# Attention in a convolution network: values for four key tiles at a time, and filler ahead of the logits in the steps between

## The chip, the core and the metric

The kernel runs on one core of a Trainium2 chip. The metric is the time of one execution on the device in microseconds (us), given as the median of several runs. The core has five engines, each with its own instruction queue: TensorE (PE; its weight loads are listed apart as PEld), VectorE (DVE), ScalarE (ACT), GpSimd (POOL) and SyncE (SP), which here issues nearly all transfers. Matmul results go to PSUM, everything else on the core is held in SBUF.

## What is computed

Eight images of 512 channels and 32 x 32 pixels pass through two layers, in fp32. The first holds nearly all the work: a 1x1 convolution, two blocks of 3x3 convolution and attention, and a closing 1x1 convolution over all intermediate results. The second is a 1x1 convolution whose weights are masked and permuted. Cut to what matters:

```python
def bot_attention(x, qkv_w, rw, rh):          # 4 heads of 64 channels, hw = 1024 pixels
    qkv = conv2d(x, qkv_w, 0).reshape(b, 3, HEADS, HD, hw)
    q, k, v = (qkv[:, 0], qkv[:, 1], qkv[:, 2])
    r = (rw + rh).reshape(1, HEADS, HD, hw)
    logits = jnp.einsum('bhdi,bhdj->bhij', q, k + r) * HD ** (-0.5)
    a = jax.nn.softmax(logits, axis=-1)
    out = jnp.einsum('bhij,bhdj->bhdi', a, v)
    return out.reshape(b, c, h, w)

t = cbs(x, cv1_w, cv1_bn, 0)                  # cbs: convolution, batch norm, silu
ys = [t[:, :C], t[:, C:]]                     # C = 256
for i in range(N):                            # N = 2 blocks
    yi = ys[-1]
    z = cbs(yi, m_cv1_w[i], m_cv1_bn[i], 1)   # 3x3
    z = bot_attention(z, m_qkv_w[i], m_rw[i], m_rh[i])
    z = jax.nn.silu(bn_eval(conv2d(z, m_cv2_w[i], 0), m_cv2_bn[i]))
    ys.append(yi + z)
return cbs(jnp.concatenate(ys, axis=1), cv2_w, cv2_bn, 0)

x = x + _L0_conv_ref(_gn(x), ...)             # _gn: group norm
x = x + _L1_conv_ref(_gn(x), ...)
```

## The kernel before

**Units.** Attention is cut into 64 units: 16 slots (an image and a block each, two images in turn) of four units, one for each pair of heads and half of the queries (512). A unit has `KT` = 8 key tiles of 128 keys. For each tile and head:

- `logits` (L487): a matmul with 64 rows for each of the two heads into a PSUM bank `lg`, a ScalarE copy of it to the SBUF tile `st` (L500), and on VectorE the running maximum `mx` (L505), read from the same bank.
- `top` (L507) transposes the maxima on TensorE (`mt`) and reduces them on VectorE; `spread` (L516) spreads them over a PSUM tile `mb` by eight more transposes.
- `soften` (L523): VectorE adds `mb` to `st`, ScalarE takes the exponential in place, and POOL sums it into `acc`, in two instructions.
- `values` (L533): a matmul for each head, with 64 output columns, added up over the eight tiles in the one bank `po`.
- `finish` (L545): the denominators `den` by a matmul with ones from `acc`, copied to `rb` by ScalarE; `divide` (L554) takes reciprocals and multiplies `po` into `q`, in two parts.

A group of `logits` uses 64 rows of TensorE's array for each head, and a group of `values` or `den` 64 columns; all other matmuls use it as 128 by 128.

**The loop** (L981 to L1036). A unit `u` goes through its eight tiles in four steps of two (`t` = 0, 2, 4, 6). Each step softens two tiles of `u`, takes the values of the two tiles softened a step before, and computes two tiles of the logits of the next unit, `nxt`. The last two tiles' values come after the loop. The reciprocals of the unit before lie in step 0.

**Filler.** The convolutions of other images and blocks fill TensorE between these pieces. `slot_filler` lists a slot's share of them as generators with estimated costs; `advance` takes pieces until the share `(base + ...) / steps` of the slot's total is reached, where `steps` is 40, ten for each unit. A piece is 1.33 or 1.72 us of the planner's time, or a little less. `clock.tick` moves the planner's clock, which decides when timed VectorE work (the transforms of the 3x3 convolution, L244, the group norms) is written into the program. The additions of `soften`, the maxima and the transforms keep their written order on VectorE (`in_turn`, L182); otherwise the framework orders each engine's instructions by its own plan of when they are ready.

**Buffers.** PSUM has eight banks here: two for `mb`, one for `po`, and five in the pool `ps_f` for logits, transposes, denominators and filler. `st` has ten buffers: eight for the unit under way and two for the next one's first logits; later logits use those that `values` and POOL's sums have released. The pool `wp` has four buffers for convolution weights (`weights`, L80), `wt` three for temporaries of the transforms. `kvp` has three for `k` and three for `v`. Batch norm parameters, the positions `rw` and `rh`, and the inputs of the second layer's mask have tiles of their own (L86 to L89), `tri` too (L658).

Of the kernel before, what the change touches and what calls it, by code (L numbers as in the profile page):

```python
# [15 lines left out]
F32 = mybir.dt.float32  # L16
# [6 lines left out]
P = 128  # L23
NB = 8
CT = 4
IT = 2
F = 32
HW = F * F
HALF = 512
NBLK = 2  # L30
HD = 64
NG = 16
KT = 8
NGR = 17

BN_CV1, BN_CV2, BN_M1, BN_M2, BN_ALL = 0, 4, 8, 12, 16
# [3 lines left out]
def conv_preact_kernel(ctx: ExitStack, tc: tile.TileContext, x, cv1, cv2, mcv1, qkv, mcv2, bn, rw, rh, conv, s_in, t_in, out):  # L40
# [3 lines left out]
    def pool(name, bufs, **kw):  # L44
        return ctx.enter_context(tc.tile_pool(name=name, bufs=bufs, **kw))

    const = pool("const", 1)
    dram = pool("dram", 1, space=bass.MemoryType.DRAM)
    small = pool("small", 2)
    qp = pool("qp", 2)  # L50
    kp_ = pool("kvp", 3)
    stp = pool("stp", 10)
    one = pool("one", 1)
    wp = pool("wp", 4)
    gx = pool("gx", 4)
    wm = pool("wm", 1)
    gy = pool("gy", 4)
    gr = pool("gr", 2)
    tp = pool("tp", 3)
    wt = pool("wt", 3)  # L60
    ps_m = pool("ps_m", 1, space=PSUM)
    ps_o = pool("ps_o", 1, space=PSUM)
    ps_f = pool("ps_f", 5, space=PSUM)
# [7 lines left out]
    def half_tile(name):  # L71
        return tp.tile([P, HALF], F32, tag="t", name=name)
# [10 lines left out]
        return t  # L83


    bn_sb = const.tile([P, 4, BN_ALL], F32, name="bn_sb")  # L86
    s_sb = const.tile([P, 2, CT, NG], F32, name="s_sb")
    rw_sb = const.tile([P, NBLK, IT, F], F32, name="rw_sb")
    rh_sb = const.tile([P, NBLK, IT, F], F32, name="rh_sb")  # L89


    w_m1 = [[dram.tile([P, IT, IT, 3, P], F32, name=f"w_m1_{i}_{r}") for r in range(6)] for i in range(NBLK)]
# [515 lines left out]
    def last_weights():  # L608
# [46 lines left out]

        yield

        tri = small.tile([P, P], F32, tag="tri", bufs=1, name="tri")  # L658
        nc.gpsimd.affine_select(
            out=tri, in_=ones, pattern=[[1, P]], compare_op=ALU.is_gt, fill=0.0, base=0, channel_multiplier=-1  # L660
        )
# [28 lines left out]
        for i in range(CT):  # L690
# [5 lines left out]
            t = half_tile(f"wl_{i}")  # L696
# [35 lines left out]
    clock = Clock()  # L732
# [210 lines left out]
    first, second = images[:2]  # L943
# [16 lines left out]
    bg.prepare()  # L960
    first.transform(0, 0.0, 0.0)
    side = last_weights()
    for n, us in enumerate(first.conv3(0)):
        clock.tick(us)
# [16 lines left out]
    for s in range(len(slots)):  # L981
        needed, total, todo = slot_filler(s)
        state = {"done": 0.0}

        def filler():
            for us, g in todo:
                start = state["done"]
                for cost in g:
                    clock.tick(cost)
                    state["done"] += cost  # L990
                    yield

                state["done"] = max(state["done"], start + us)

        fill = filler()

        def advance(share):
            goal = max(share * total, min(1.0, share / 0.74) * needed + 0.1)
            while state["done"] < goal:
                if next(fill, "end") == "end":  # L1000
                    break

        steps = 4 * (KT + 2)
        for j in range(4):
            u = units[4 * s + j]
            nxt = units[4 * s + j + 1] if 4 * s + j + 1 < len(units) else None
            base = j * (KT + 2)
            u.top()
            clock.tick(0.9)
            advance((base + 1) / steps)  # L1010
            u.spread()
            clock.tick(0.9)
            advance((base + 2) / steps)
            if before:
                before.finish()
                clock.tick(0.9)
            for t in range(0, KT, 2):
                u.soften(t)
                if before and t == 0:
                    before.divide(1)  # L1020
                u.soften(t + 1)
                if t:
                    u.values(t - 2)
                    u.values(t - 1)
                    clock.tick(2.0)
                if nxt:
                    nxt.logits(t)
                    nxt.logits(t + 1)
                    clock.tick(2.0)
                advance((base + 4 + t) / steps)  # L1030
            u.values(KT - 2)
            u.values(KT - 1)
            clock.tick(2.0)
            before = u
        for _ in fill:
            pass  # L1036
# [59 lines left out]
```

## Time and profile before

| what | value |
|---|---|
| median of 3 runs | 3273.07 us |
| lowest and highest of them | 3271.97, 3283.51 us |
| profiled execution, own time | 3278.47 us |
| its span, first to last instruction | 3276.7 us |
| granted TensorE clock | 0.99 |
| HBM read, written | 317.42 MB, 79.69 MB |

The profile is of one execution. Its times are in us, unless in ns. A row of a group of instructions shows the line, the engine and operation, output and inputs, the shape and number; then the busy time of the engine and the mean ns of one instruction; then the engine's idle time just before such instructions, and what ended it. A row of the timeline shows a start, a duration, and the instructions merged in it. TensorE's ends are modelled and overlap the next start a little, so starts are what is compared. By fortieths of the span the clock is at nine tenths or more throughout. The units run from about 184 us, when the first logits start, to 3145 us; before lies the preparation of weights and the first two images, after it the last image's convolutions.

### The profile page before, as it was taken

What the parts mean: (1) busy time and instruction counts of PE and PEld (TensorE: products, weight loads), DVE (VectorE), ACT (ScalarE), POOL (GpSimd) and SP (SyncE); (2) the same over time, 40 slices, a digit from 0 to 9 for tenths busy, and PEclk for the clock granted to TensorE, in tenths of its full rate; (3) what the DMA queues carried; (4) which work ended last, traced back from release to release, by engine and by line L of the source; (5) the groups of instructions that cost most, each with busy time, mean ns of one, the idle gap of its engine ahead of it and who ended that gap; (6) DMA issues with size and microseconds to landing.
All of it is one profiled execution on the core that took longest, in us unless ns stands there. A gap on an engine that the chain in (4) does not pass through costs nothing.

```text
span 3276.7 us, 33257 instructions
## 1 busy us (share of the span) xinstructions
PE 3159.1 (96%) x11716; PEld 1538.0 (47%) x11716; DVE 2045.9 (62%) x2717; ACT 1756.6 (54%) x2369; POOL 1219.1 (37%) x971
## 2 busy tenths in 40 slices
PE   7999999998999999999999999999999999999998
PEld 3645345353545445354545445354445444453343
DVE  5436566666666575767666675767656676666642
ACT  3245765854545655644545555644655554646631
POOL 2104433335334343344334343444334433444420
PEclk9999999999999999999999999999999999999999
DMA  8752352330323241423323341423333341423366
GB/s 292 275 171 71 119 170 94 116 106 20 121 98 106 75 148 55 161 84 106 122 98 105 104 144 54 161 84 108 124 105 108 101 141 49 160 71 116 111 217 205
DMA packets 142007, 399.30 MB, mean 122 GB/s; under 512 B 13072, under 2 KB 14352, under 8 KB 141840
## 3 DMA queue, kind: packets, MB, share of 16 engines
q1 hardware_dynamic: 141120, 396.94, 36.1%
q8 instruction: 93, 1.52, 0.2%
q14 instruction: 74, 0.61, 0.1%
q10 hardware_dynamic: 720, 0.23, 0.0%
HBM read 317.42 MB, written 79.69 MB: 121 GB/s over the span
## 4 chain that ended last, share of the span: by engine, by line
PE 69%; DVE 11%; issue 5%; ACT 4%; DMA 4%; POOL 1%; POOLq 0%; SPq 0%; ACTq 0%; DVEq 0%
PE cv L175 14%; PE m L297 12%; PE po L537 11%; PE lg L494 10%; PE qk L175 6%; PE l L175 5%; PE v L389 3%; DVE st L525 3%; PE mt L513 2%; PE m L175 2%; DVE rb L556 2%; DVE mx L505 2%; PE den L549 2%; PE mb L521 2%; DMA x<-in_x 1%
## 5 line engine op out<-in xcount | busy, mean ns | idle before, releaser
L531 POOL TENSOR_TENSOR sum<-sum,st 128x512 f32<-128x512 f32 x768 | 973.9, 1299 | 771.5 <-ACT st L526 771.5
L526 ACT ACTIVATE st<-st 128x1024 f32<-128x1024 f32 x512 | 534.3, 1056 | 471.4 <-DVE st L525 464.8
L505 DVE TENSOR_TENSOR mx<-mx,lg 128x512 f32<-128x512 f32 x768 | 479.3, 681 | 434.1 <-ACT st L500 433.6
L500 ACT COPY st<-lg 128x512 f32<-128x512 f32 x1024 | 528.1, 594 | 246.1 <-PE lg L494 189.9
L525 DVE TENSOR_TENSOR st<-st,mb 128x1024 f32<-128x1024 f32 x512 | 604.2, 1213 | 79.8 <-PE mb L521 79.8
L297 PE MATMUL m<-plane,w_m 128*128 128x256 f32 x2304 | 534.0, 386 | 18.0 <-DVE z L351 8.3
L494 PE MATMUL lg<-q,k 64*128 64x512 f32 x2048 | 534.6, 618 | 10.4 <-ACT rb L551 3.3
L537 PE MATMUL po<-st,v 128*64 128x512 f32 x2048 | 509.5, 609 | 17.2 <-ACT st L526 11.4
L297 PEld LDWEIGHTS m<-plane,w_m 128*128 128x128 f32 x2304 | 431.4, 191 | 142.7 <-issue 40.8
L531 POOL TENSOR_TENSOR sum<-st,st 128x512 f32<-128x512 f32 x128 | 162.2, 1288 | 834.1 <-ACT st L526 712.0
L175 PE MATMUL cv<-y,w_cv 128*128 128x512 f32 x1024 | 466.5, 600 | 4.9 <-DVE mx L505 2.1
L494 PEld LDWEIGHTS lg<-q,k 64*128 64x128 f32 x2048 | 188.9, 186 | 346.2 <-issue 236.5
L175 PEld LDWEIGHTS cv<-y,w_cv 128*128 128x128 f32 x1024 | 185.5, 190 | 252.0 <-issue 231.6
L537 PEld LDWEIGHTS po<-st,v 128*64 128x64 f32 x2048 | 125.2, 136 | 327.6 <-issue 231.6
L556 DVE RECIPROCAL rb<-rb 128x256 f32<-128x256 f32 x128 | 216.1, 1725 | 66.0 <-ACT rb L551 66.0
L175 PE MATMUL cv<-x,w_cv 128*128 128x512 f32 x512 | 242.2, 622 | 12.3 <-DVE mx L505 4.1
L175 PE MATMUL l<-x,w_l 128*128 128x512 f32 x512 | 235.2, 604 | 9.6 <-DVE mx L505 6.2
L175 PE MATMUL qk<-z,w_qkv 128*128 128x512 f32 x512 | 234.2, 600 | 1.6 <-DVE mx L505 1.6
L514 DVE TENSOR_REDUCE nm<-mt 128x4 f32<-128x512 f32 x128 | 83.0, 685 | 221.5 <-PE mt L513 221.2
L130 ACT ACT_TABLE_LOAD x122 | 156.5, 1283 | 14.7 <-PE m L175 6.4
L175 PEld LDWEIGHTS cv<-x,w_cv 128*128 128x128 f32 x512 | 97.0, 197 | 138.7 <-issue 112.1
L175 PEld LDWEIGHTS l<-x,w_l 128*128 128x128 f32 x512 | 93.3, 191 | 133.6 <-issue 106.5
(144 smaller groups left out, 2342.1 us busy)
## 6 DMA issues: line engine op xcount, KB each, us to landing
w_m<-w_m SPq DMA_DIRECT2D x96, 768.0 KB, 4.4
w_cv<-in_cv SPq DMA_DIRECT2D x90, 512.0 KB, 3.5
y<-y SPq DMA_DIRECT2D x64, 512.0 KB, 4.7
x<-in_x SPq DMA_DIRECT2D x56, 512.0 KB, 5.2
y<-y SPq DMA_DIRECT2D x64, 256.0 KB, 3.6
k<-r SPq DMA_DIRECT2D x32, 512.0 KB, 3.8
res<-y SPq DMA_DIRECT2D x32, 512.0 KB, 4.2
xr<-in_x SPq DMA_DIRECT2D x32, 512.0 KB, 4.3
```

What stands on the lines that cost most here:

```text
L130: nc.scalar.activation(dst, src, AF.Silu, bias=bn_b[:, col : col + 1], scale=bn_s[:, col : col + 1])
L175: nc.tensor.matmul(ps, w, moving, start=(n == 0), stop=(n == len(terms) - 1))
L297: nc.tensor.matmul(ps[:, ts(co, 256)].rearrange("p (t x) -> p t x", x=F), w[:, co, c, dx], u[:, 9 * c : 9 * c + 8, dx : dx + F], start=(j ...
L389: nc.tensor.matmul(ps[:, ts(j, P)], z[:, c, ts(4 * j4 + j, P)], w[:, c, 512 + P * hp : 512 + P * hp + P], start=(c == 0), stop=(c == IT - 1),)
L494: nc.tensor.matmul(lg[h], self.k[r, ts(t, P)], self.q[r, self.hp, ts(self.half, HALF)], start=True, stop=True)
L500: nc.scalar.copy(st[:, h], lg[h])
L505: in_turn(nc.vector.tensor_tensor(self.mx[:, h], so_far[:, h], lg[h], ALU.max))
L525: in_turn(nc.vector.tensor_tensor(st, st, flat(self.mb), ALU.add))
L526: nc.scalar.activation(st, st, AF.Exp)
L531: nc.gpsimd.tensor_tensor(self.acc[:, h], so_far[:, h], self.st[t][:, h], ALU.add)
L537: nc.tensor.matmul(self.po[HD * h : HD * h + HD], self.v[:, t, ts(h, HD)], self.st[t][:, h], start=(t == 0), stop=(t == KT - 1),)
L556: nc.vector.reciprocal(self.rb[:, r], self.rb[:, r])
```

## The change

Values are taken in two groups of four tiles: tiles 0 to 3 in step `t` = 4, tiles 4 to 7 after the last step. In the other steps an additional `advance` stands between `soften` and `logits`, to the share `base + 2.8 + t`; the `advance` after the logits keeps its goal. `st` gets twelve buffers, `wp` three instead of four, `wt` two instead of three. The small parameters move into one tile `par`, which takes one of the three `k` buffers.

```diff
-    stp = pool("stp", 10)
+    stp = pool("stp", 12)
-    wp = pool("wp", 4)
+    wp = pool("wp", 3)
-    wt = pool("wt", 3)
+    wt = pool("wt", 2)
...
-    bn_sb = const.tile([P, 4, BN_ALL], F32, name="bn_sb")
-    s_sb = const.tile([P, 2, CT, NG], F32, name="s_sb")
-    rw_sb = const.tile([P, NBLK, IT, F], F32, name="rw_sb")
-    rh_sb = const.tile([P, NBLK, IT, F], F32, name="rh_sb")
+    par = kp_.tile([P, HW], F32, tag="k", name="par")
+
+    def param(first, shape):
+
+        return par[:, first : first + P].rearrange("p (a b c) -> p a b c", b=shape[0], c=shape[1])
+
+    s_sb = param(0, (CT, NG))
+    rw_sb = param(128, (IT, F))
+    rh_sb = param(256, (IT, F))
+    bn_sb = par[:, 512 : 512 + 4 * BN_ALL].rearrange("p (a b) -> p a b", b=BN_ALL)
...
-        tri = small.tile([P, P], F32, tag="tri", bufs=1, name="tri")
+        tri = par[:, 384:512]
...
                 u.soften(t + 1)
-                if t:
-                    u.values(t - 2)
-                    u.values(t - 1)
-                    clock.tick(2.0)
+                if t == KT // 2:
+                    for key in range(KT // 2):
+                        u.values(key)
+                    clock.tick(4.0)
+                else:
+
+                    advance((base + 2.8 + t) / steps)
                 if nxt:
                     nxt.logits(t)
                     nxt.logits(t + 1)
                     clock.tick(2.0)
                 advance((base + 4 + t) / steps)
-            u.values(KT - 2)
-            u.values(KT - 1)
-            clock.tick(2.0)
+            for key in range(KT // 2, KT):
+                u.values(key)
+            clock.tick(4.0)
```

## The prediction

> **What bounds the kernel now.** I read the page's busy totals first, then its chain, then the groups of TensorE by line and form, then TensorE's timeline.
>
> ```profile
> PE 3159.1 (96%) x11716; PEld 1538.0 (47%) x11716; DVE 2045.9 (62%) x2717; ACT 1756.6 (54%) x2369; POOL 1219.1 (37%) x971
> ...
> PE 69%; DVE 11%; issue 5%; ACT 4%; DMA 4%; POOL 1%; POOLq 0%; SPq 0%; ACTq 0%; DVEq 0%
> ```
>
> TensorE is busy 96% of the span, and no other engine passes 62%. The chain runs through TensorE for 69%. So a microsecond counts here if TensorE loses it: as idle time, or inside its busy time.
>
> ```profile
> L494 PE MATMUL lg<-q,k 64*128 64x512 f32 x2048 | 534.6, 618 | 10.4 <-ACT rb L551 3.3 <-ACT y L130 3.1 <-ACT st L500 3.0
> L297 PE MATMUL m<-plane,w_m 128*128 128x256 f32 x2304 | 534.0, 386 | 18.0 <-DVE z L351 8.3 <-DVE mx L505 6.2 <-DMA w_m<-w_m 2.8
> L537 PE MATMUL po<-st,v 128*64 128x512 f32 x2048 | 509.5, 609 | 17.2 <-ACT st L526 11.4 <-DVE q L558 5.8
> ...
> L513 PE MATMUL mt<-ident,mx 128*128 128x128 f32 x512 | 73.3, 288 | 10.7 <-DVE mx L505 10.7
> ```
>
> The last column is TensorE's idle time before a group, by who ended it. Values (po) waited 17.2 us, logits (lg) 10.4, the transposes of the maxima (mt) 10.7. Adding all such idle times of the timeline between 250 us, where the units run, and the end gives 85 us.
>
> ```profile
> 1596.36 1.94 PE L537 MATMUL po<-st,v 128*64 128x512 f32 x8
> 1598.23 1.99 PE L494 MATMUL lg<-q,k 64*128 64x512 f32 x8
> 1600.15 5.45 PE L297 MATMUL m<-plane,w_m 128*128 128x256 f32 x24
> 1605.53 1.94 PE L537 MATMUL po<-st,v 128*64 128x512 f32 x8
> ```
>
> Each matmul is two records. A filler group of twelve 128x512 records takes 5.35 us from its start to the next group's (1609.31 to 1614.66), one of eight 3.63 (1528.12 to 1531.75), so a record is 0.43 us of work (I use 0.427), and one of 256 columns half of it, 0.213; the two heads of values or logits share the array, so eight records are 4 x 0.427 = 1.71 us of work. Starts are 1.87 us apart from values to logits (0.16 over), 1.92 from logits to filler (0.21 over), 5.38 from filler to values against 24 x 0.213 = 5.12 (0.26 over). So every change of tile shape costs 0.16 to 0.26 us, unseen as idle time. Beyond that, groups get broken up:
>
> ```profile
> 1500.81 1.12 PE L494 MATMUL lg<-q,k 64*128 64x512 f32 x2
> 1501.86 1.08 PE L537 MATMUL po<-st,v 128*64 128x512 f32 x4
> 1502.87 1.12 PE L494 MATMUL lg<-q,k 64*128 64x512 f32 x2
> 1503.94 1.08 PE L537 MATMUL po<-st,v 128*64 128x512 f32 x4
> 1504.95 1.13 PE L494 MATMUL lg<-q,k 64*128 64x512 f32 x4
> ```
>
> One step's values and logits take from 1500.81 to 1506.01, 5.20 us where 3.79 is usual: lone heads no longer share the array.
>
> **What the Trainium skill says.** "TensorEngine Tiling (Array Packing)", Key Properties: changing the tiling mode drains TensorE, changing only the tile doesn't. The trace agrees: 0.16 to 0.26 us per change, as above. "PSUM — Partial Sum Buffer", Specifications, gives 8 banks per partition; the kernel's pools take all eight (mb two, po one, five shared), and logits of two tiles need four of the five. "TensorE: Matmul & The Clock Gate", the specification table, has VectorE and ScalarE work as strict queues. The trace agrees: at 1543.28 values start late (0.69 us) behind VectorE's reciprocals and `q`, and logits' maxima come after those.
>
> **The change part by part.** There are 64 units (16 slots of four); I cost 63, since the last has no logits beside it.
>
> *Fewer, longer values groups.* Work is the same. Per unit two filler→values changes (0.25 each) and two values→logits changes (0.16) go: -0.82. Step 0 loses denominator→logits (0.15, from 1.01 between starts against 0.85) and gains denominator→filler (taken as 0.16, the price of leaving the same tile shape). Steps 0, 2 and 6 gain filler→logits: 0.21 (filler of six 128x256 records at 1539.74, logits at 1541.23: 1.49 against 1.28). Added 0.79, removed 0.97: -0.18 a unit. With 0.23 for filler→values it is -0.14; I take -0.16 x 63 = **-10 us**. The bounds are -0.4 (the filler ahead of logits in step 0 comes out empty) and 0: -25 to 0 us. I expect it not empty: 0.8 of 40 steps of some 103 us is 2.06 us, above the largest single piece of 1.72.
>
> *Waits of values.* Values of tiles 0 to 3 now stand in step 4, one step (about 9 us by the timeline) or two behind their exponentials, and po is written a step later than `divide`, which frees it. All 17.2 us of waits before po go. Of logits' waits, those on `rb` (filler now lies after the denominators) and on `st` (its buffer is freed two steps ahead instead of just before, also by POOL's sums, for which ScalarE waited 41.3 us) are 6.3 us. Filler's waits on the maxima are 20.9 us over its groups, on `st` 4.0: a filler that follows logits finds all banks held. The filler there shrinks from 2 shares to 1.2 in three of four steps, so half goes: 12.5. Sum 36; TensorE reaches VectorE's next backlog sooner, so I take five sixths: **-30 us**, bounds -36 and -12 (every wait on VectorE comes back later).
>
> *Broken groups.* In the timeline logits run straight into values 24 times (0.5 over), into logits after a hold 11 times (0.7), values into filler 18 times (0.38): 12 + 8 + 7 = 27 us over the sum of their work, of which ordinary changes would keep a little. They come from values or a bank not being ready in the planned order. Values no longer are late; logits' banks may be. **-15 us**, bounds -25 and +10.
>
> *Logits straight after filler.* This is new: until now 1.87 us of values lay between filler and logits in 191 cases, in which ScalarE or VectorE could empty filler's last bank. Logits need four of five banks; where filler stops in mid-sum it holds one, and the bank that it finished 1.3 to 1.7 us before must be empty when the fourth logits matmul starts, 0.85 us later. ScalarE has the step's exponentials (1.06 us each) and perhaps a 1.28 us table load ahead of that. Filler stops so at perhaps a quarter of the 3 x 63 = 189 places (sums of two quanta half the time, of four a quarter, none where a bank is one quantum). 45 places by about 0.3 us: **+15 us**, bounds 0 and +95 (0.5 us at all 189). What stands behind a waiting logits matmul on TensorE is everything.
>
> *Maxima to transposes.* Filler between logits(6,7) and the next `top` shrinks from 2 shares (5.15 us) to 1.2 (3.1), values grow by 1.7: some 0.35 us less for ScalarE's four copies (0.59) and VectorE's four maxima (0.68). mt waited three times by 3.6 us. **+4 us**, bounds -5 and +15. Timed VectorE work (the transforms) falls due around other instructions, since the planner's clock moves by 4.0 twice instead of by 2.0 four times; it is within these bounds.
>
> *Buffers and queues.* No DMA is added; filler's loads and stores move with its pieces on SP by at most one step's share, and POOL's sums keep their place in POOL's queue. Three weight buffers instead of four let a load start one weight later. From SP's issue times of the 250 weight loads, what remains is two weights of use: about 9 us at least while units run, against 4.4 us median to landing, so it stays covered; after 3145 us, without units, 6 us at two places: **+1 us**, up to +8. Two `wt` tiles instead of three are written and read by VectorE in its own order: nothing. The parameters' tile holds one of three `k` buffers until the positions and ranks are made, before the loop takes the third: nothing. Twelve `st` tiles may let the weights' preparation run ahead (TensorE waited 2.8 us for them at 78 and 85 us): **-1 us**.
>
> Sum: -10 - 30 - 15 + 15 + 4 + 1 - 1 = **-36 us**. The profiled execution took 3278.47 us (span 3276.7, 1.8 around it); it becomes 3242.5. The median of the runs is 5.4 below the profiled one: 3273.07 - 36 = **3237 us**.
>
> **Rivals.** *Nearly all of it comes through:* waits -36, broken groups -25, changes -10, logits after filler +5: -66, **3207 us**. For it speaks that few waits need more than a microsecond of slack; against, that VectorE at 62% carries the same work. *The gain is given back:* a third of the waits, and the new bank waits at +20, broken groups unchanged: -10 - 12 + 20 + 4 = +2, **3275 us**. For it: most of the 85 us is filler waiting on itself (z, y, m2s) and on maxima. *Slower:* one mechanism, filler's last bank at the head of logits. Its place is the 189 filler→logits passages; against the other terms' -51 us it decides from a mean of 0.27 us on. At 0.45 us it costs 85: +34, **3307 us**. For it: logits waited 3.1 us once for `y`, and filler→logits occurs only 11 times before, so its price is hardly seen; against: those 11 show no idle time. *The change doesn't do what it says*, the pieces ahead of logits being empty: changes -25, but logits of tiles 0 and 2 come within 5.2 us with no values between, bank waits +30, so -25 - 25 - 10 + 30 = -30, **3243 us**, not to be told from the forecast by time.
>
> **How the numbers follow.** A measurement here can tell 0.5%, 16 us, from no change. Forecast 0.46 (its own range 3215 to 3257); nearly all 0.16; empty pieces 0.06; given back 0.14; slower 0.18. Faster by over 16 us: 0.46 + 0.16 + 0.06 = 0.68, within 0.14, slower 0.18. Leaving a tenth at each end: 3198 to 3295.
>
> **What would show it.** After: values in about 128 groups instead of 269, mostly of 16 records; po's idle near nothing; filler's idle on mx about 10 us; TensorE's busy total down by some 20 us or more at unchanged instruction counts. Wrong, if logits' idle grows beyond 20 us, with `y`, `cv2s`, `x2r` or `m2s` named, if lone heads of logits are more frequent, or if mt's idle goes beyond 25 us.

## The result, and the profile after

| what | before | after |
|---|---|---|
| median, same comparison, 7 runs each | 3276.68 us | 3290.81 us |
| ratio, 95% interval | | 1.0042 (1.0027 to 1.0056) |
| span of the profiled execution | 3276.7 us | 3288.6 us |
| first transposes of maxima (first unit ready) | 218.2 us | 231.7 us |
| from there to the last unit's transposes | 2894 us | 2892 us |
| from those to the end | 164.4 us | 164.6 us |

The change costs 14 us, 0.42%, where 36 us less was forecast. The three stretches of the last rows are read from TensorE's timeline. The whole difference of the spans, 11.9 us, lies ahead of the first transposes (+13.5). The loop, which was to become about 36 us shorter, took the same time.

The busy totals and the chain of the page after:

```profile
PE 3173.9 (97%) x11716; PEld 1547.1 (47%) x11716; DVE 2059.5 (63%) x2717; ACT 1749.0 (53%) x2361; POOL 1231.0 (37%) x971
...
PE 70%; DVE 10%; issue 6%; ACT 5%; DMA 2%; POOL 1%; SPq 0%; POOLq 0%; DVEq 0%; ACTq 0%
```

TensorE has the same 11,716 instructions and is busy 14.8 us longer, 7.5 of it ahead of the first transposes (196.1 us before, 203.7 after). Its groups by line and form, after (line numbers are six higher than before in this part of the file):

```profile
L500 PE MATMUL lg<-q,k 64*128 64x512 f32 x2048 | 546.8, 619 | 12.1 <-DVE mx L511 3.9 <-ACT cv2s L136 3.9 <-DVE x2r L477 1.5
L303 PE MATMUL m<-plane,w_m 128*128 128x256 f32 x2304 | 535.9, 385 | 6.9 <-DVE x2r L477 2.4 <-DMA w_m<-w_m 2.0 <-DVE z L357 1.2
L543 PE MATMUL po<-st,v 128*64 128x512 f32 x2048 | 500.3, 603 | 15.8 <-DVE q L564 11.4 <-ACT st L532 4.4
...
L181 PE MATMUL cv<-x,w_cv 128*128 128x512 f32 x512 | 242.3, 620 | 19.7 <-ACT y L136 6.8 <-DVE mx L511 5.3 <-DMA w_cv<-in_cv 5.3
...
L181 PE MATMUL m<-q,w_m 128*128 128x512 f32 x256 | 125.1, 626 | 10.8 <-ACT m2s L136 10.8
...
L519 PE MATMUL mt<-ident,mx 128*128 128x128 f32 x512 | 70.1, 280 | 0.0
```

Idle time went where it was looked for and came in elsewhere. The transposes (`mt`) wait no more (10.7 before), and the values' wait on `st` fell from 11.4 to 4.4 us. But the values' wait on `q`, the division that frees `po`, rose from 5.8 to 11.4, and the matmuls `m<-q`, which waited 4.0 us before and only for `st`, now wait 10.8 us, all for `m2s`: ScalarE's copy of filler's finished bank. `cv<-x` shows a wait for a weight load (5.3 us) that it did not have. The rows of these two before:

```profile
L175 PE MATMUL cv<-x,w_cv 128*128 128x512 f32 x512 | 242.2, 622 | 12.3 <-DVE mx L505 4.1 <-ACT y L130 4.0 <-ACT x L165 2.4
L175 PE MATMUL m<-q,w_m 128*128 128x512 f32 x256 | 121.4, 614 | 4.0 <-ACT st L500 4.0
```

For the loop, from the first to the last unit's transposes, I split what TensorE's records show beyond their own work into three. A record's work is 0.427 us for 512 columns, and half of that for logits, values and denominators, of which two share the array.

- *Idle* is the sum of its waits in the timeline.
- *Half clock* is time lost because the granted clock fell to 0.5. The traces show such stretches, 3.41 us long or a multiple of that; in the trace after, a 128x512 record takes 0.853 us in them (median) and 0.429 elsewhere. I count half of TensorE's busy time in these stretches, which is an estimate. The profile counts it as busy, and a fortieth of the span averages it away. In this stretch after, ahead of the loop, the mean granted clock is 0.70 (the columns are length, busy time and number of instructions for PE, PEld, DVE, ACT and POOL, the clock, and DMA):

```profile
208.40:214.00 5.60, 5.51 (x10) 2.21 (x12) 3.85 (x6) 2.70 (x7) 0.00 (x0) 0.70 0.14 51
```

- *Changes and breaks* is all the rest: shape changes and broken groups.

| in the loop | idle | half clock | changes and breaks | sum |
|---|---|---|---|---|
| before | 83.9 us | 25.0 us | 236.7 us | 345.6 us |
| after | 75.6 us | 16.7 us | 253.3 us | 345.6 us |

Changes and breaks grew by 17 us, and that repeats: a second execution of the kernel before has 81.8, 23.0 and 237.8 us, and one with the same loop as the changed kernel ("weights later" below) 72.8, 13.6 and 254.7. What grew are groups of logits or values with an odd number of matmuls, so that one head goes without its partner: 30 before, 80 after. After, a group of 6 records takes 1.93 us, as long as one of 8 (1.92), and one of 2 takes 1.05, as long as one of 4 (1.07). So 50 more of them cost some 21 us (50 x 0.427), while 60 fewer changes of shape at 0.2 us give back 12. Both are estimates from these figures; 8 of the 17 us stay unexplained.

By cause, the idle time on `mx` fell from 32.7 to 15.5, and on the exponentials from 11.4 to 4.4. On ScalarE's three copies of filler (`m2s`, `y`, `cv2s`) it rose from 8.3 to 25.6, and on `q` from 5.8 to 11.4. So 24 us of such waits went, and 23 us of others came.

Where in a unit the sum stands (the first stretch starts with the transposes of the maxima; each ends with the named logits, and the last with the start of the next transposes):

| stretch of a unit, all units | before | after |
|---|---|---|
| transposes to the first step's logits | 81.5 us | 103.2 us |
| to the second step's | 74.5 us | 61.9 us |
| to the third's | 65.2 us | 71.5 us |
| to the fourth's | 71.4 us | 69.8 us |
| to the next transposes | 53.1 us | 39.1 us |

The last stretch, in which four tiles' values stand instead of two, gains 14 us, and the second 13. The first, where filler now comes ahead of the logits, loses 22, and the third, with four tiles' values, 6.

TensorE's timeline in the middle of the loop, after, shows what became of the groups:

```profile
1036.19 3.70 PE L181 MATMUL m<-q,w_m 128*128 128x512 f32 x8
1039.83 1.98 PE L500 MATMUL lg<-q,k 64*128 64x512 f32 x6
1042.81 1.04 PE L543 MATMUL po<-st,v 128*64 128x512 f32 x2 [1.00 <-DVE q L564]
1043.78 1.12 PE L500 MATMUL lg<-q,k 64*128 64x512 f32 x2
1044.84 1.98 PE L181 MATMUL m<-q,w_m 128*128 128x512 f32 x4
...
1054.05 3.65 PE L543 MATMUL po<-st,v 128*64 128x512 f32 x14
```

This is step 0 of a unit: filler, then logits. Only three of the four logits matmuls run (x6, two records each), and they take as long as four. Then comes one matmul of the values that belong to step 4, drawn forward by two steps. It waits 1.00 us for the division of the unit before, and so does everything behind it. The fourth logits matmul follows alone, and the values at 1054.05 have 14 records left instead of 16. In the program's order on TensorE, whole groups of four tiles' values are 99 of 128, and values come in 163 groups (271 before); changes of shape fell only from 936 to 876.

### The profile page after: what moved, and what is told of

Its sections match the earlier page's. It is cut to its first block, busy times and chain, and to the rows that moved or that the text cites. A ratio compares the mean times of both kernels' runs of the same rounds, so it can differ in the third digit from the quotient of the medians.

```text
span 3288.6 us, 33211 instructions
## 1 busy us (share of the span) xinstructions
PE 3173.9 (97%) x11716; PEld 1547.1 (47%) x11716; DVE 2059.5 (63%) x2717; ACT 1749.0 (53%) x2361; POOL 1231.0 (37%) x971
## 4 chain that ended last, share of the span: by engine, by line
PE 70%; DVE 10%; issue 6%; ACT 5%; DMA 2%; POOL 1%; SPq 0%; POOLq 0%; DVEq 0%; ACTq 0%
PE m L303 13%; PE cv L181 12%; PE po L543 12%; PE lg L500 11%; PE qk L181 6%; PE l L181 5%; PE v L395 3%; DVE st L531 3%; DVE rb L562 2%; PE m L181 2%; PE mt L519 2%; PE den L555 2%; PE mb L527 2%; ACT st L532 1%; DVE mx L511 1%
## 5 line engine op out<-in xcount | busy, mean ns | idle before, releaser
L531 DVE TENSOR_TENSOR st<-st,mb 128x1024 f32<-128x1024 f32 x512 | 604.7, 1214 | 76.8 <-PE mb L527 76.8
L500 PE MATMUL lg<-q,k 64*128 64x512 f32 x2048 | 546.8, 619 | 12.1 <-DVE mx L511 3.9
L543 PE MATMUL po<-st,v 128*64 128x512 f32 x2048 | 500.3, 603 | 15.8 <-DVE q L564 11.4
L543 PEld LDWEIGHTS po<-st,v 128*64 128x64 f32 x2048 | 139.6, 137 | 332.1 <-issue 279.5
L562 DVE RECIPROCAL rb<-rb 128x256 f32<-128x256 f32 x128 | 216.3, 1726 | 53.2 <-ACT rb L557 53.1
```

The source lines that it names most:

```text
L500: nc.tensor.matmul(lg[h], self.k[r, ts(t, P)], self.q[r, self.hp, ts(self.half, HALF)], start=True, stop=True)
L531: in_turn(nc.vector.tensor_tensor(st, st, flat(self.mb), ALU.add))
L543: nc.tensor.matmul(self.po[HD * h : HD * h + HD], self.v[:, t, ts(h, HD)], self.st[t][:, h], start=(t == 0), stop=(t == KT - 1),)
L562: nc.vector.reciprocal(self.rb[:, r], self.rb[:, r])
```

## The experiments

Each was compared with runs of the kernel before on the same chip; a ratio below 1 is faster than before. The profiled execution of a kernel can lie some us from its median, and loop times are of that one execution. "Changes" are changes of tile shape in the program's order on TensorE, from the first values on. The time lost in the loop is given as idle + half clock + changes and breaks. Two executions of the kernel before differ by 3 us in the loop.

### Which part costs the time

Four kernels: the kernel before with all the buffer changes and the single parameters' tile; with the third weight buffer alone; the changed kernel without the additional filler; and the changed kernel with values in twos as before, but with the additional filler.

```diff
 e1  # the buffers and `par` as changed; values and filler as before
 e2  # before, and only
-    wp = pool("wp", 4)
+    wp = pool("wp", 3)
 e3  # changed, without
-                else:
-                    advance((base + 2.8 + t) / steps)
 e4  # changed, with
+                if t != KT // 2:
+                    advance((base + 2.8 + t) / steps)
+                if t:
+                    u.values(t - 2)
+                    u.values(t - 1)
```

> Kernel before with all buffer changes (twelve st, three weight buffers, two wt, the parameters in one tile), but its own order of values and filler. In the changed kernel the first maxima's transposes start at 231.7 us instead of 218.2, and from there to the end the two kernels differ by under 2 us. Theory A: the loss is the start, and the buffers cause it: first transposes at 228 to 232 us, time 10 to 14 us over before (3286 to 3291). Rival R: the start's lateness is chance (TensorE's clock warming up at other moments), and the loop's new order costs the time: first transposes at 218 to 222 us, time within 4 us of before.

> Kernel before with three weight buffers instead of four, nothing else. Theory A, with the third buffer as the cause: the second w_cv load of the stage before the loop is issued after 155 us instead of at 121, TensorE waits some 5 us for it, first transposes at 225 to 232 us, time 7 to 14 us over before. Theory B (the shared tile of parameters, or twelve st, shift the start): first transposes within 3 us of 218, time within 3 us of before.

> Changed kernel without the additional filler ahead of the logits: values in fours, all filler after the logits. Its program has 822 changes of tile shape on TensorE from the first values on, against 876 in the changed kernel and 936 before. If changes of shape at 0.2 us set the loop's time: 54 x 0.2 = 11 us below the changed kernel, about 3280, that is 23 us below before once the start's 13 us are taken off. If logits that follow each other within 5 us wait for banks (what the filler was put in to avoid): logits' and filler's idle on maxima up by 20 to 60 us and time 3295 to 3340.

> Changed buffers, values in twos as before, but the filler split, with a piece ahead of values and logits in three of four steps. 983 changes of shape against 936 before: 47 x 0.2 = 9 us over the kernel that has the new buffers alone. If filler ahead of the logits removes waits on maxima and on rb, as forecast (12 to 19 us), it comes out 3 to 10 us below that kernel; if it only cuts groups up, 9 to 15 us above.

| kernel | median us | ratio (95%) | first transposes | loop | lost in the loop | changes |
|---|---|---|---|---|---|---|
| before | 3278.25 | 1 | 218.2 | 2894 | 83.9 + 25.0 + 236.7 | 936 |
| buffers | 3278.03 | 1.0002 (0.9992 to 1.0011) | 230.3 | 2885 | 77.7 + 19.2 + 239.8 | 936 |
| `wp` alone | 3280.09 | 1.0005 (0.9996 to 1.0014) | 231.5 | 2885 | 75.0 + 24.9 + 236.7 | 936 |
| values grouped | 3289.68 | 1.0041 (1.0025 to 1.0057) | 230.5 | 2893 | 83.2 + 15.7 + 246.9 | 822 |
| filler split | 3303.14 | 1.0076 (1.0054 to 1.0097) | 231.4 | 2907 | 83.2 + 23.7 + 253.2 | 983 |

The late start is the third weight buffer's: it alone moves the first transposes by 13 us. Where it comes from stands in the profile after. SyncE's queue, after:

```profile
160.96 0.32 SPq L78 DMA_DIRECT2D w_m<-gf  x1
161.37 0.94 SPq L78 DMA_DIRECT2D r<-r  x2
162.41 1.14 SPq L78 DMA_DIRECT2D w_cv<-in_cv  x1
```

and TensorE's timeline, after:

```profile
156.85 7.03 PE L181 MATMUL cv<-x,w_cv 128*128 128x512 f32 x16
169.14 5.06 PE L181 MATMUL cv<-x,w_cv 128*128 128x512 f32 x8 [5.25 <-DMA w_cv<-in_cv]
174.03 0.28 PE L152 MATMUL gm_a<-mv_a,gmat 128*128 128x4 f32 x2
```

The second `w_cv` of this stage is issued at 162.41 us, behind the stores of the second block's weights (`w_m<-...`). The kernel before issues that load at 121.44:

```profile
121.44 0.33 SPq L78 DMA_DIRECT2D w_cv<-in_cv  x1
```

TensorE then stands for 5.25 us, and its next eight records take 4.89 us, from 169.14 to 174.03, where eight take 3.63 otherwise. TensorE was behind by 4.6 us at 156.85 already; the kernel before started this group at 152.21:

```profile
152.21 10.46 PE L175 MATMUL cv<-x,w_cv 128*128 128x512 f32 x24
```

Up to there the changed kernel had 13.65 us at half clock and the kernel before 6.83, which by itself costs some 3.4 of the 4.6 us. A later wait of 2.07 us, 0.28 longer than the same one before, is followed by eight slow records (1.7 us more). Together 13.1 of the 13.5 us.

But the late start doesn't decide the time by itself, as I had expected it to (3286 to 3291 us with all the buffer changes): the kernels with the old order of the loop win 6 to 9 us back in it (2885 against 2894 and 2891) and end where they were. In both, idle time is lower. With `wp` alone neither half clock nor changes and breaks differ from before. With all the buffer changes less time passes at half clock, and values wait 5.8 us on `st` instead of 11.4:

```profile
L543 PE MATMUL po<-st,v 128*64 128x512 f32 x2048 | 510.7, 610 | 11.7 <-ACT st L532 5.8 <-DVE q L564 5.8
```

(The line numbers are those of the changed kernel here, too.) The grouping alone has 114 changes of shape fewer than before and still loses 10 us more to changes and breaks (246.9 us), so it pays elsewhere what it saves in regular changes. The additional filler alone is the worst of the four, 25 us above the kernel with the buffers, where I had expected at most 15: it was the part of the change that I had counted as a gain for the waits.

### Does the order cause it, or the start

Four kernels: before once more, for the spread; the changed kernel and the kernel before with the logits' and values' matmuls kept in their written order by scheduling edges, which add no instruction; and the changed kernel with the preparation of the second block's weights, whose stores stood ahead of the load, moved behind the filler that uses it.

```diff
 e5, e7
+        def pe_in_turn(instruction):  # each logits and values matmul after the one written before it
+            if pe_turn:
+                tc.add_manual_dep(instruction.ins, pe_turn.pop().ins.name, IN_ORDER, reason="order of TensorE")
+            pe_turn.append(instruction)
 e6
-    transform_weights(1)
     positions(1)
     clock.run(bg.take(7.0, force=True))
+    transform_weights(1)
```

> The kernel before once more, for a second profile. The kernels with three weight buffers had their first transposes at 230 to 232 us, the one profile of before at 218.2, but their medians equal that of before. If the 12 us at the start are a property of the buffers: 217 to 220 us again, and the loop (first to last transposes) 3058 less 159, that is 2894 us as before. If the one profile was an early chance: 225 to 232 us, and a loop near 2885 us.

> Changed kernel, with the matmuls of logits and values kept among themselves in the order in which they are written (a scheduling edge from each to the next, no wait on the chip, since all are on TensorE). In the changed kernel the plan draws values forward into logits that have no bank yet: 14 logits groups of one matmul, values before `divide` has freed po. Theory: these broken groups ate the gain. Shape changes go from 876 to 843, po's idle on q from 11.4 to under 3 us, time 15 to 30 us below the changed kernel (3261 to 3276). Rival: the places are short of a bank either way, and TensorE waits there instead: logits' idle up by 10 to 20 us, time within 8 us of the changed kernel.

> The kernel before with the same edges. Shape changes 936 to 911. If broken groups cost as the working had it (0.4 to 0.7 us each, 43 of them): 8 to 15 us below before, 3263 to 3270. If TensorE waits there instead: within 5 us of before.

> Changed kernel with the second block's weights prepared after the convolution that stands before the loop, so that the load of its second w_cv is queued ahead of the weights' stores on SP. The program of the loop on TensorE is the same. If the start counts: TensorE's wait of 5.3 us on w_cv goes, first transposes 6 to 10 us earlier (222 to 226), time 6 to 10 us below the changed kernel (3281 to 3285). If a late start is made up for later in the loop, as it looked in the kernels with buffers alone: time within 4 us of the changed kernel.

| kernel | median us | ratio (95%) | loop | lost in the loop | changes |
|---|---|---|---|---|---|
| before again | 3277.43 | one run | 2891 | 81.8 + 23.0 + 237.8 | 936 |
| changed, in order | 3293.41 | 1.0051 (1.0036 to 1.0066) | 2893 | 83.6 + 21.1 + 241.6 | 843 |
| before, in order | 3266.83 | 0.9968 (0.9955 to 0.9981) | 2880 | 87.0 + 22.2 + 222.2 | 911 |
| changed, weights later | 3281.14 | 1.0013 (1.0006 to 1.0021) | 2888 | 72.8 + 13.6 + 254.7 | 876 |

The groups of the changed kernel in order:

```profile
L508 PE MATMUL lg<-q,k 64*128 64x512 f32 x2048 | 544.4, 619 | 22.8 <-DVE mx L519 11.6 <-ACT m2s L136 3.5 <-ACT cv2s L136 3.0
...
L551 PE MATMUL po<-st,v 128*64 128x512 f32 x2048 | 490.9, 603 | 0.0
...
L181 PE MATMUL cv<-x,w_cv 128*128 128x512 f32 x512 | 245.0, 626 | 25.1 <-ACT y L136 9.8 <-DVE mx L519 6.6 <-DMA w_cv<-in_cv 5.5
...
L181 PE MATMUL m<-q,w_m 128*128 128x512 f32 x256 | 125.0, 626 | 14.1 <-ACT m2s L136 14.1
```

No values are drawn forward, and they don't wait at all (0.0). Changes and breaks fall by 12 us, but in their place logits wait 22.8 us, and filler longer on `y` and `m2s`. The time is no better than the changed kernel's own (the intervals overlap). So keeping the order is not enough to have the gain: what was lost in broken groups is lost in waiting instead.

In the kernel before the same edges gain 10 us: there its values still wait (27.6 us in the row), but fewer groups are broken (10 with a lone head instead of 30), and changes and breaks fall by 14.5 us.

```profile
L502 PE MATMUL lg<-q,k 64*128 64x512 f32 x2048 | 521.4, 618 | 6.5 <-ACT rb L559 3.3 <-ACT y L130 3.1
L545 PE MATMUL po<-st,v 128*64 128x512 f32 x2048 | 508.2, 611 | 27.6 <-DVE q L566 13.9 <-ACT st L534 13.4
```

With the weights later that load is issued at 149.12 us, TensorE doesn't wait for it, the first transposes come at 221.7 us, and the changed kernel is 9.5 us faster than it was against the kernel before (14.1 to 4.4 us over it in median, each in its own comparison). About two thirds of the measured loss is the start; the loop still gains little or nothing by the change (2888 us in this execution, against 2894 and 2891 before).

### Can another order have the gain

Four kernels, all with the weights later: the second step's additional filler with a later goal, so that logits are spaced evenly; the additional filler taken to the end of a sum, so that it holds no half-done bank when logits start; the order of before with the changed buffers, in order; and values grouped without the additional filler, in order.

```diff
 e13
-                    advance((base + 2.8 + t) / steps)
+                    advance((base + (3.5 if t == 2 else 2.8) + t) / steps)
 e10
-                    advance((base + 2.8 + t) / steps)
+                    advance((base + 2.8 + t) / steps, whole=True)  # on to the last matmul of a bank; marks in the filler are left out here
 e11  # e1 with pe_in_turn and the weights later
 e12  # e3 with pe_in_turn and the weights later
```

> The changed kernel with the early w_cv load (late weights), and the filler ahead of step 2's logits taken to share base + 5.5 instead of base + 4.8; the filler after them still goes to base + 6. So the logits of tiles 0 and 2 are on average 1.8 us further apart and those of 2 and 4 nearer by as much. In the changed kernel the mean distance fell from 8.9 to 7.7 us, and TensorE's idle time between logits 0 and 4 rose from 23 to 38 us over the loop. Theory: logits that follow within some 8 us find ScalarE and VectorE still at work on the step before, and filler's banks wait behind that. Then the idle between logits 0 and 4 falls by 5 to 15 us, and the time is 5 to 15 us below the kernel with the late weights alone (3266 to 3276). Rival: the wait moves to logits 4; time within 4 us of it.

> The changed kernel with late weights, with filler ahead of logits taken on to the end of a sum, so that it holds no bank over the logits (and often uses up the filler meant for after them). Theory of the forecast: a bank held by a half-finished sum is what logits lack; then logits' idle and the groups cut up fall and the time is 5 to 15 us below the kernel with late weights alone. Rival: the plan itself still has 17 lone logits matmuls (14 before), so it isn't the held bank; with no filler after logits, maxima and exponentials are waited for: 5 to 40 us above.

> Order of the kernel before (values in twos, no filler ahead of logits) with the new buffers, the late weights, and the edges that keep logits and values in written order. If the gains add up: first transposes at 220 to 223 us, loop 2876 to 2880 us, time 3255 to 3263. If the buffers' shorter loop was only the making up for the late start: loop as with the edges alone, 3264 to 3268.

> Values in fours without filler ahead of logits, late weights, and the edges: 800 changes of shape, the fewest of all (911 in the order before with edges). If changes of shape set the time: 111 x 0.2 = 22 us below the order before with edges, about 3240. If banks do, as the experiment with values in fours has it: 3270 to 3285.

| kernel | median us | ratio (95%) | lost in the loop | changes |
|---|---|---|---|---|
| spaced evenly | 3296.36 | 1.0045 (1.0030 to 1.0060) | 82.9 + 21.5 + 244.0 | 850 |
| whole sums | 3290.23 | 1.0031 (1.0018 to 1.0043) | 76.0 + 23.0 + 256.3 | 821 |
| old order, new buffers, in order | 3271.13 | 0.9970 (0.9960 to 0.9979) | 86.9 + 22.8 + 225.0 | 911 |
| grouped, in order | 3288.30 | 1.0027 (1.0015 to 1.0038) | 85.4 + 24.8 + 240.6 | 800 |

The forecast had named half-done banks at the head of logits as the danger. Removing them (whole sums) doesn't help, so they aren't the cause alone; but this kernel also has less filler left after the logits. Spacing moves the wait: between the third and the fourth step's logits idle time grows from 18 to 42 us while others fall. The old order, kept, is as good with the changed buffers as without them, 9 us under the kernel before. The orders with values grouped, with 800 to 876 changes, lose 341 to 355 us in the loop, the old order kept loses 331 and 335 with more changes (911). So the number of changes doesn't set the time. All of these kernels have a pool of five banks, of which two tiles' logits take four; whether that is what the grouped orders lack is tested next.

### Is it the banks

First by leaving work out. In these four kernels the maxima are not spread and not subtracted (`st` is added to itself, so that VectorE keeps its instruction), and `mb` has no banks. The two banks stay unused (n5) or go to the shared pool (n7); each as the kernel before and as the changed kernel with the weights later, so that in these pairs the buffers differ too.

```diff
-            in_turn(nc.vector.tensor_tensor(st, st, flat(self.mb), ALU.add))
+            in_turn(nc.vector.tensor_tensor(st, st, st, ALU.add))
-            u.spread()
-    ps_m = pool("ps_m", 1, space=PSUM)
-    ps_f = pool("ps_f", 5, space=PSUM)
+    ps_f = pool("ps_f", 7, space=PSUM)   # 5 in n5
```

> Leaves out that the maxima are spread and subtracted (the eight transposes into mb, and mb as the addend: `soften` adds st to itself, so VectorE's instruction stays), which frees mb's two banks; they stay unused here, five banks in the shared pool. Order of the kernel before. It is the measure for the other three. 64 x 0.97 us of transposes go: 3190 to 3230.

> The same cut in the changed kernel with late weights, five shared banks. Both theories: within 10 us of the order before with five banks, as with the whole kernels (4 us apart).

> The same cut, order of the kernel before, with the two freed banks in the shared pool: seven. The plan has 899 changes of shape against 906. Theory that banks hold the loop up: idle of TensorE on maxima falls, 5 to 20 us below five banks. Theory that VectorE's and ScalarE's work between softmax and logits does it: within 5 us.

> The same cut in the changed kernel with late weights, seven shared banks. The plan has 798 changes of shape against 825, and 126 whole groups of four tiles' values against 105. Theory that the shortage of banks took the forecast gain: 20 to 40 us below the order before with seven banks (fewer changes and waits come through), idle on m2s, y, cv2s, q and maxima under half. Rival, that the gain is gone for another reason (VectorE and ScalarE are behind whatever the banks): within 8 us of the order before with seven banks.

Then with nothing left out. The maxima are spread through two banks of a shared pool of seven, ScalarE copies them to SBUF as bf16, and VectorE adds them from there; once with the changed order, once with that of before (both with the changed buffers and the weights later).

```diff
-            self.mb = pair(ps_m, "mb", f"mb_{self.name}")
+            self.mb = mbp.tile([P, 2, HALF], mybir.dt.bfloat16, tag="mb", name=f"mb_{self.name}")
             for h in range(2):
+                ps = bank(f"mbp_{self.name}_{h}")
                 for c in range(4):
-                    nc.tensor.transpose(self.mb[:, h, ts(c, P)], ...)
+                    nc.tensor.transpose(ps[:, ts(c, P)], ...)
+                nc.scalar.copy(self.mb[:, h], ps)
```

> The whole computation in the changed order with late weights: the spread maxima go through two banks of the shared pool, which now has seven, and ScalarE copies them to SBUF as bf16 (128 copies of some 0.6 us), from where VectorE adds them. If banks took the gain: 35 to 65 us below the kernel before (3210 to 3245), and 20 to 40 us below the order in twos with seven banks. If the copies' place in ScalarE's queue and the longer way from maxima to additions eat it: within 15 us of before.

> The same with values in twos and no filler ahead of logits (the order before). If seven banks help either order: 15 to 40 us below before (3240 to 3262), still 20 to 40 above values in fours with seven banks. If banks matter to the changed order alone: within 10 us of before.

| shared banks | order of before: us, ratio (95%) | changed order: us, ratio (95%) | difference |
|---|---|---|---|
| 5, maxima left out | 3241.57, 0.9882 (0.9864 to 0.9900) | 3219.69, 0.9813 (0.9798 to 0.9828) | -22 us |
| 7, maxima left out | 3186.50, 0.9709 (0.9691 to 0.9727) | 3149.40, 0.9598 (0.9577 to 0.9618) | -37 us |
| 7, whole computation | 3239.51, 0.9868 (0.9852 to 0.9883) | 3201.12, 0.9755 (0.9734 to 0.9775) | -38 us |

With seven banks the changed order gains 37 and 38 us, the size of the forecast. In the whole computation TensorE loses in the loop 55.6 us idle, 17.1 to half clock and 195.0 to changes and breaks, against 68.3, 26.9 and 212.7 with the order of before: idle time and changes and breaks both fall, as the forecast had it. The first step, which lost 22 us with five banks, now loses 3 (61.1 to 64.5). 125 of the 128 groups of values stay whole (99 with five banks), 2 groups have a lone head (80 with five banks, 34 with seven and the order of before), and there are 802 changes. The changed order with seven banks is faster than both kernels of this case, 81 us below the one before, more than the 35 to 65 expected.

With five banks and the maxima left out the changed order gained 22 us already. I had expected less than 10, so banks aren't all. That a unit's first steps then don't wait for the spread maxima may be what lets part of the gain through; it is not shown. Two more banks alone then bring 55 us to the order of before (5 to 20 expected) and 70 us to the changed one. So the change gains its full size with seven banks, whether the maxima are left out or not; with five it gains a part of it without them, and nothing with them.

The kernels with seven banks and the whole computation differ from the others in more than banks. The additions read the maxima from SBUF and take 1384 ns each instead of 1214, and ScalarE has 69 us of copies more. Both cost time, so neither explains the gain by itself. The same way through SBUF with five shared banks was not run.

TensorE's groups with seven banks and the changed order, whole computation:

```profile
L500 PE MATMUL lg<-q,k 64*128 64x512 f32 x2048 | 526.0, 619 | 6.6 <-DVE mx L511 6.1 <-ACT y L136 0.3
L545 PE MATMUL po<-st,v 128*64 128x512 f32 x2048 | 473.5, 602 | 10.9 <-ACT st L534 9.4 <-DVE q L566 1.3
...
L181 PE MATMUL m<-q,w_m 128*128 128x512 f32 x256 | 120.1, 605 | 2.9 <-ACT m2s L136 2.0 <-DVE q L566 0.8
...
L519 PE MATMUL mt<-ident,mx 128*128 128x128 f32 x512 | 74.3, 286 | 20.5 <-DVE mx L511 20.5
```

The waits on `m2s`, `y` and `cv2s` are nearly gone: 10.8 became 2.0 in `m<-q`. The values take 473.5 us instead of 500.3 for the same 2048 records. What waits longest in these rows now is `mt`, 20.5 us on VectorE's maxima. The timeline has the groups as they were written:

```profile
1627.10 5.42 PE L181 MATMUL cv<-y,w_cv 128*128 128x512 f32 x12
1632.45 1.99 PE L500 MATMUL lg<-q,k 64*128 64x512 f32 x8
1634.37 3.70 PE L181 MATMUL cv<-y,w_cv 128*128 128x512 f32 x8
1638.00 3.65 PE L545 MATMUL po<-st,v 128*64 128x512 f32 x16
1641.58 1.99 PE L500 MATMUL lg<-q,k 64*128 64x512 f32 x8
```

Filler, four logits, filler, eight values matmuls, four logits, without a break or a wait. With seven banks and the order of before, values wait three times as long, for `q` above all; there `po` is written a step earlier:

```profile
L545 PE MATMUL po<-st,v 128*64 128x512 f32 x2048 | 510.2, 615 | 32.6 <-DVE q L566 21.8 <-ACT st L534 10.6
```

## Why the prediction was wrong

The direction was wrong: 3237 us was forecast, 36 below the 3273; it came out 14 us above its own comparison's 3277. Two steps failed: the broken groups in the loop, and the buffers at the start.

- **Broken groups (-15).** This is the step that failed in the loop. The forecast took broken groups to come from "values or a bank not being ready in the planned order", and expected relief from values being ready early. With five banks they became more: groups with a lone head rose from 30 to 80, and changes and breaks together, forecast at -25, rose by 17 us. In the timeline, values that are ready early are drawn forward between logits, as at 1042.81. Kept from that, the kernel waits for `m2s`, `y` and `mx` instead, and loses as much (346.3 us in the loop, against 345.6 as changed and 345.6 before). That a missing bank is the reason for each such place is argued. What is shown is that with seven banks the same order has 2 such groups and loses 267.7 us, against 307.9 for the order of before with seven. So the forecast was a fair price of the change where banks are not short, and it was written down for a place where they are; some luck is in that agreement, for 10 of these 40 us are half clock, for which it had no term. The prediction had said that logits of two tiles need four of five banks, and gave it a price in one term only, *logits straight after filler*.
- **Waits of values (-30).** All waits before `po` were to go (17.2 us); 15.8 stayed, because the wait on `q` doubled, for values drawn forward ahead of the division (with the order kept it is gone). The other parts came near: filler's waits on the maxima fell from 20.9 to 11.6 us (half was forecast), and logits no longer wait on `rb`.
- **Logits straight after filler (+15).** Logits' idle rose by only 1.7 us (10.4 to 12.1). The price is paid by filler: idle on `m2s`, `y` and `cv2s` rose by 17 us. That is near the +15 in size, but not at the place that was priced. The bank that filler held in mid-sum isn't decisive (whole sums: no gain). Taken together, the three terms of waiting were forecast at -11 us, and idle time fell by 8.3. The sum is near by luck, since its parts are not.
- **Changes of shape (-10).** The program's order has 60 fewer (936 to 876), and 802 where the groups stay whole, with seven banks. At 0.16 to 0.26 us 60 changes are 10 to 16 us, the forecast's size, but the lone heads cost more than that.
- **Maxima to transposes (+4).** Wrong in sign: `mt` waited 10.7 us before, 0.0 after. The way from the last logits to the transposes did get shorter, as forecast (7.38 to 6.78 us in the mean); why the maxima were ready all the same stays open.
- **Buffers (+1, up to +8).** This is the second step that failed, a term put far too low: the start came 13.5 us later, and moving the weights' stores behind the load gave the changed kernel 9.5 us back. I had looked at weight loads while units run and at the end, not at the preparation, where the weight stores lie ahead of the loads on SyncE. There what counted was less the transfer's time than what stood before it in the queue.
- **Which rival.** *Given back* (3275 us) came nearest in time, but it left broken groups unchanged. *Slower* had the right resource, the fourth bank, at a wrong place. The signs named beforehand point the same way: lone heads of logits are more frequent (14 lone matmuls instead of 10), `cv2s` and `x2r` now stand in logits' row though its idle stays under 20 us, values aren't near nothing (15.8 us), and TensorE's busy time rose by 14.8 us instead of falling by 20. Busy time has in it changes and breaks and half clock.

What stays open: why the kernels with the old order win back 6 to 9 of the 13 us lost at the start, and the changed kernel doesn't; how much of the gain with seven banks is the banks' alone, since with the maxima left out five banks gave 22 us of it; and which single wait stands behind each of the values drawn forward, since the trace names the releaser of a wait but not the bank that a matmul was not planned for.

## What to carry to other kernels

A gain in changes or waits can be taken only where the order can be kept without new waits: count the buffers that the new order holds at once, PSUM banks first. Add up idle time and broken groups together, because here one turned into the other when the order was kept, and take time at a lower clock out of both. When fewer buffers of a pool look harmless in the steady loop, look at the start too, and at what stands ahead of the load in its queue. Where an order is limited by a scarce resource, test it once with the resource enlarged, even by leaving work out: this helps to tell whether the order or the resource is at fault. If leaving work out changes the answer by itself, as here, test it also with nothing left out.

## What the runs showed of the hardware

- With five shared banks, the time that TensorE loses in the loop doesn't follow the number of shape changes: 345.6 us with 936 (before), 345.8 with 822 (grouping alone), 355.3 with 821 (whole sums), 331.4 with 911 (before, in order). With seven banks it was 267.7 with 802.
- A lone head costs as much as a pair: after, groups of 6 records took 1.93 us and of 8 1.92, of 14 3.58 and of 16 3.59.
- "TensorE: Matmul & The Clock Gate", What's actually happening, has TensorE's clock throttled again after an idle window of about 3.4 us. The trace after agrees at the start: after a wait of 5.25 us eight records take 4.89 us instead of 3.63. A wait of 2.07 us just later (until 208.49 us) is followed by eight records in 5.33 us too, at a granted clock of 0.70. Waits of 2.14 us (all the buffer changes) and 2.11 us (values grouped) at the same place are not followed by a lower clock. So a shorter wait can come before a throttled stretch, and what decides is not shown.
